# Self attention of a perceiver layer on one core: a tile's row maxima and their way through DRAM directly behind its scores, its subtraction one iteration later, the transposes of the quantized rows later

## The chip, the cores and the metric

The program runs on one core of a Trainium2 chip. The metric is the device time of one execution in microseconds (us); lower is better. TensorE does the matmuls (PE in the profile, PEld its weight loads), VectorE is DVE, ScalarE is ACT, GpSimd is POOL, and SyncE issues most of the DMAs (its queue is SPq).

## The reference

x is 16 batches x 64 queries x 1024. Three residual layers follow one another, each on the layernorm of x:

```
x = x + xattn(layernorm(x), ctx)   # 16 x 1024 context rows, 32 query heads, 8 key/value heads
x = x + attn(layernorm(x))         # self attention: bias, rope, 64 keys per batch
x = x + ffn(layernorm(x))          # int4 rows, ternary weights, relu(gate)^2 * up, int8 rows, down
```

The change lies in the self attention, `softmax(q k^T / sqrt(32)) v` over 64 queries and 64 keys of each batch and head. The feed forward layer begins with this on every row of its input:

```
beta = mean(abs(x)); xq = clip(round(x * sqrt(7) / (beta + eps)), -8, 7)
```

and its gate and up products have 2752 columns each.

## The kernel before

The 1024 rows are eight tiles of 128 (two batches each). The order of all instructions is written out by hand (`tc.manual_schedule()`): each engine, and each DMA queue, works its instructions off in the order in which the program calls them. Work for TensorE that can go anywhere stands as closures in a list, `fillers`; `fill()` (L1055) runs the next one.

The loop of the self attention (L1255) has nine iterations, t = 0 to 8. In iteration t, `two` is tile t and `last` is tile t-1. What the calls issue:

- `by_key(t)` (L773): 32 small matmuls into `w`, four PSUM banks, then two ACT copies (L791) to the tile's 2048 scores per row in SBUF.
- `maxima(t)` (L797), in two halves: a DVE transpose of 32x32 blocks into `blocks2` (L800) and a DVE reduction (L801). What is subtracted in the end is one number for each column (a head and a query), the maximum over the keys, which lie on the partitions.
- `row(t)` (L808): eight small DVE transposes (L813), a small reduction (L817), then on SP's queue a DMA to DRAM (L821) and two DMAs that spread it back over the partitions into `shift2` (L825), 512 KB each. `shift2` lies in the place of `blocks2`.
- `subtract(t)` (L829): one DVE instruction (L830) that waits for those DMAs. `exponentials(t)` (L832): one ACT instruction (L833), in place.
- `values(t)` (L835): 64 matmuls into `w` (L841, L852), which need the exponentials; then three ACT copies.
- `finish(t)` (L868): twelve transposes on TensorE, a DVE reciprocal (L878), two DVE multiplications (L883), and one POOL addition to the residual (L889).
- `quantize(t)` (L912) gives four pieces for the feed forward layer's input, all of them mainly on DVE: `statistics` (L187 to L191, with a power on POOL, L193), `magnitude` (L179, L921), `scaled` (L924 to L927), `rounded` (L930, L932, and the small POOL operations L933, L934). The rounded tile has one buffer.
- `transpose3(t)` (L938): eight TensorE transposes of the rounded tile (L941) into one of two PSUM banks "t0" and "t1", which take turns, and an ACT copy (L942) to `xqT[t]`.

The fillers in iterations 0 to 3 are those of the projection of the second half of the rows: four half chunks of keys, four value steps, then sixteen half chunks of queries, called q1 to q16 below. After each second half a chunk goes through `rotary` (L712): ACT L719, DVE L720 and L721, POOL L722 and L723. From iteration 4 the fillers are 32 gate/up steps (`gate_up`, L952), called g0 to g31: sixteen matmuls each, three ACT operations (L967, L969, L970) and a POOL multiplication (L971). The first twelve go by tiles 0 and 1, then tile 2, then tile 3, each with the column chunks 0 to 2, so that g6 is the first of tile 2, g9 the first of tile 3, and g12 the first of chunk 3. After a chunk's step on tile 3 (g9, g10, g11, g15, ...) `fetch` puts the weights of the chunk three later on SP's queue (L949), two DMAs of 344 KB into the buffers just left. So g12 needs the fetch that is issued behind g9.

Both kinds of filler take PSUM banks from `four_tile` (L94), which goes round m0, m1, t0, t1. An even gate/up step takes t1 and m0, an odd one m1 and t0. Counted through the code, the turns give `transpose3(2)` t0 and `transpose3(5)` t1, before and after the change.

How one iteration runs over these calls, for t from 1 to 7 (two halves of one line each):

```
by_key(t) | fill | exponentials(t-1), maxima(t, 0) | fill | transpose3(t-2), values(t-1), maxima(t, 1) | fill
finish(t-1), row(t) | then fill and a piece of quantize(t-1), three or four times, subtract(t) behind the second piece
```

For t up to 4 there are three of these last steps (all four pieces are issued), later four. In iteration 5 `transpose3(3)` stands behind the first fill. From iteration 1 on, q1 to q6 fall into iteration 1, q7 to q12 into 2, q13 to q16 into 3. Two gate/up steps stand ahead of `by_key(4)`; g2 to g7 follow in iteration 4, g8 to g14 in 5, g15 to g21 in 6, g22 to g28 in 7, g29 to g31 in 8. Behind the loop come the remaining gate/up steps, with the pieces of `quantize(7)` and other work at fixed numbers of steps (`beside`, L1321), among them `transpose3(7)` behind step 8 (L1325); step 9 is the first that uses its tile.

Of the kernel before, what the change touches and what calls it, by code (L numbers as in the profile page):

```python
# [25 lines left out]
NT = B * NQ // P  # L26
# [23 lines left out]
def kernel(  # L50
# [33 lines left out]
    def t_tile(shape, dtype, name, n=None):  # L84

        turns["t"] ^= 1
        n = turns["t"] if n is None else n
        return ps_t.tile(shape, dtype, tag=f"t{n}", name=name)
# [5 lines left out]
    def four_tile(name):  # L94

        turns["four"] = (turns["four"] + 1) % 4
        if turns["four"] < 2:
            return ps_m.tile([P, 512], F32, tag=f"m{turns['four']}", name=name)
        return t_tile([P, 512], F32, name, turns["four"] - 2)
# [812 lines left out]
    def quantize(t):  # L912

        xn = place(xn3_at, [DIM])
        statistics, normalize = layernorm(xn, xs[t], f"n3_{t}")
        b = beta[:, t : t + 1]
        rb = small.tile([P, 1], F32, tag="rb", name=f"rb_{t}")

        def magnitude():
            normalize()  # L920
            nc.vector.tensor_reduce(b, xn, AX.X, ALU.add, apply_absolute_value=True)  # L921

        def scaled():
            nc.vector.tensor_scalar_mul(b, b, 1.0 / DIM)  # L924
            nc.vector.tensor_scalar_add(rb, b, EPS)
            nc.vector.reciprocal(rb, rb)
            nc.vector.tensor_scalar(xn, xn, SQRT7, rb, ALU.mult, ALU.mult)  # L927

        def rounded():
            nc.vector.tensor_scalar(xn, xn, -8.0, 7.0, ALU.max, ALU.min)  # L930
            xq3[t] = place(xq_at, [DIM], BF)
            nc.vector.tensor_scalar(xq3[t], xn, MAGIC, MAGIC, ALU.add, ALU.subtract)  # L932
            nc.gpsimd.tensor_tensor(cgate[:, t : t + 1], b, wscale[:, 0:1], ALU.mult)  # L933
            nc.gpsimd.tensor_tensor(cup[:, t : t + 1], b, wscale[:, 1:2], ALU.mult)  # L934

        return [statistics, magnitude, scaled, rounded]

    def transpose3(t):  # L938
        tp = t_tile([P, KC, P], BF, f"xqp_{t}")
        for k in range(KC):  # L940
            nc.tensor.transpose(tp[:, k, :], xq3[t][:, bass.ts(k, P)], ident_b)  # L941
        nc.scalar.copy(xqT[t], tp)  # L942

    def fetch(n):

        wbs[n] = []
        for i in range(2):
            q = wb_ring.next([KC, CW], F8)
            nc.sync.dma_start(q.rearrange("p k o -> p (k o)"), ternary[i][n % NCH])  # L949
            wbs[n].append(q)  # L950

    def gate_up(n, t, banks, scalar=False):  # L952

        c = n % NCH
        relu, prod = relu_ring.next([CW]), prod_ring.next([CW])
        for i in range(2):
            ps = banks(i)
            for k in range(KC):
                nc.tensor.matmul(  # L959
                    ps[:, :CW],  # L960
                    lhsT=xqT[t][:, k, :],
                    rhs=wbs[n][i][:, k, :],
                    start=(k == 0),
                    stop=(k == KC - 1),
                )
            if i == 0:
                nc.scalar.activation(relu, ps[:, :CW], AF.Relu, scale=cgate[:, t : t + 1])  # L967
        if scalar:
            nc.scalar.activation(prod, ps[:, :CW], AF.Copy, scale=cup[:, t : t + 1])  # L969
            nc.scalar.activation(relu, relu, AF.Square)  # L970
            nc.gpsimd.tensor_tensor(inter[t][:, bass.ts(c, CW)], prod, relu, ALU.mult)  # L971
            return
        nc.vector.scalar_tensor_tensor(
            prod, ps[:, :CW], cup[:, t : t + 1], relu, ALU.mult, ALU.mult
        )
        nc.gpsimd.tensor_tensor(inter[t][:, bass.ts(c, CW)], prod, relu, ALU.mult)
# [78 lines left out]
    def fill(n=1):  # L1055
        for _ in range(n):
            if fillers:
                fillers.pop(0)()

    with tc.manual_schedule():  # L1060
# [14 lines left out]
        unit, last = Unit(0, kT, v), None  # L1075
# [22 lines left out]
        for n in range(2 * B):  # L1098
# [27 lines left out]
            for i in range(4):  # L1126
# [25 lines left out]
                t = n // 4 - 1  # L1152
# [62 lines left out]
            last, unit = unit, following  # L1215
# [38 lines left out]
        two, last = None, None  # L1254
        for t in range(NT + 1):  # L1255
            two, last = (Tile2(t, w) if t < NT else None), two
            late = t >= NT // 2
            if t == NT // 2 - 2:
                for n in range(2):
                    fetch(n)  # L1260
            if t == NT // 2:
                fill(len(fillers))
                fetch(2)
                steps = [(n, tt) for n in range(NCH) for tt in range(NT // 2)]

                steps[:12] = [
                    (n, tt) for tiles in ((0, 1), (2,), (3,)) for n in range(3) for tt in tiles
                ]

                def beside(n, tt):  # L1270
                    gate_up(n, tt, lambda i: four_tile(f"gu_{n}_{tt}_{i}"), scalar=True)
                    if tt == NT // 2 - 1:
                        fetch(n + 3)

                fillers += [lambda s=s: beside(*s) for s in steps]
            if t == NT // 2:
                fill(2)
            pieces = quantize(t - 1) if last and two else []

            def piece():  # L1280
                if pieces:
                    pieces.pop(0)()

            if two:
                two.by_key()
            fill()
            if t == NT // 2 + 1:
                transpose3(t - 2)
            if last:
                last.exponentials()  # L1290
            if two:
                two.maxima(0)
            fill()
            if t > 1 and t != NT // 2 + 1:
                transpose3(t - 2)
            if last:
                last.values()
            if two:
                two.maxima(1)
            fill()  # L1300
            if last:
                last.finish()
            if two:
                two.row()
            for n in range(4):
                if n == 3 and two and t <= NT // 2:
                    break
                fill()
                piece()
                if n == 1 and two:  # L1310
                    two.subtract()
            while pieces:
                piece()
        fill(len(fillers))
# [6 lines left out]
        beside = {9 + 2 * i: step for i, step in enumerate(sum(map(quantize8, range(4)), []))}  # L1321
        beside[0] = fetch_down
        for i, piece in enumerate(pieces):
            beside[(1, 2, 4, 5)[i]] = piece
        beside[8] = lambda: transpose3(NT - 1)  # L1325
        for t in range(2):
            for i, step in enumerate(transpose8(t)):
                beside[14 + 8 * t + 2 * i] = step
# [94 lines left out]
```

## Time and profile before

| | us |
|---|---|
| median of 3 runs | 1886.26 (1885.81 to 1888.18) |
| the profiled execution's own time | 1885.72 |
| its span (first to last instruction) | 1883.9 |
| TensorE busy in the span | 1828.3 |
| mean granted TensorE clock | 0.991 |
| start of `by_key(1)` | 1509.1 |
| start of the last reciprocal L878 (iteration 8) | 1714.7 |

The iterations can be told apart by the DVE reciprocal L878, which comes once in each, at the end of the twelve TensorE transposes of `finish`: it starts at 1524.18, 1551.33, 1578.64, 1607.27, 1637.58, 1665.58, 1689.60 and 1714.72 us in iterations 1 to 8.

The timeline of an engine lists its instructions in order of time: the start, the time from the first start to the last end, the engine and line, what is written from what, how many there are, and in square brackets how long the engine sat idle ahead of them and which instruction released it.

### The profile page before, as it was taken

The numbers are of one execution on the slowest core, as the hardware profiler recorded it, in microseconds if no ns is written. First come the engines' busy times: TensorE is split into PE (matmuls) and PEld (weight loads), VectorE is DVE, ScalarE is ACT, GpSimd is POOL, SyncE is SP. The second block draws the span as 40 slices with busy tenths as digits, with TensorE's granted clock in tenths as the row PEclk, the third lists the DMA queues.
The fourth block names the chain that finished last, engine by engine and source line by source line (L and its number), as shares of the span: only waits on it lengthen the run. The fifth ranks groups of instructions, "written<-read, shape, count | busy, mean of one in ns | idle before, by whom it ended". The sixth has DMA issues, their size and how long they took to land.

```text
span 1883.9 us, 26367 instructions
## 1 busy us (share of the span) xinstructions
PE 1828.3 (97%) x10880; PEld 1083.4 (58%) x10880; DVE 1224.9 (65%) x1436; ACT 928.1 (49%) x988; POOL 872.5 (46%) x479
## 2 busy tenths in 40 slices
PE   8999999999899999999999999999999998889999
PEld 5445556565565665666666666664445544555654
DVE  3012688777777887878878878877523377565564
ACT  1233666656566766766766766543100134563221
POOL 1000457646574674674674665664412334334420
PEclk9999999999999999999999999999999999899999
DMA  9234569777677877877877867743020022334201
GB/s 342 75 103 149 183 226 268 210 242 252 167 241 219 258 227 222 257 228 226 252 227 231 250 224 212 193 174 150 5 89 0 12 65 61 72 88 126 73 29 51
DMA packets 65928, 314.65 MB, mean 167 GB/s; under 512 B 10192, under 2 KB 19344, under 8 KB 49040
## 3 DMA queue, kind: packets, MB, share of 16 engines
q1 hardware_dynamic: 56592, 252.15, 38.2%
q0 software_dynamic: 8064, 58.72, 15.6%
q10 hardware_dynamic: 1152, 2.10, 0.3%
q8 instruction: 85, 1.39, 0.3%
q14 instruction: 35, 0.29, 0.0%
HBM read 293.74 MB, written 19.20 MB: 166 GB/s over the span
## 4 chain that ended last, share of the span: by engine, by line
PE 65%; DVE 4%; DMA 3%; issue 1%; ACT 1%; POOL 0%; SPq 0%; DVEq 0%; POOLq 0%; ACTq 0%
PE v L426 16%; PE z L407 10%; PE wo L250 6%; PE t L575 5%; PE o L637 5%; PE d L1038 4%; PE q L250 4%; PE g L959 4%; PE p L407 4%; DMA arena<-tops 2%; PE k L250 1%; PE v L740 1%; PE gu L959 1%; DVE arena L830 1%; PE w L841 1%
## 5 line engine op out<-in xcount | busy, mean ns | idle before, releaser
L628 POOL TENSOR_TENSOR arena<-arena 128x1024 f32<-128x1024 f32 x192 | 541.9, 2822 | 20.5 <-ACT arena L619 8.5
L426 PE MATMUL v<-arena 128*128 128x256 f32 x1792 | 405.2, 382 | 1.2 <-ACT arena L442 1.2
L594 DVE TENSOR_TENSOR arena<-t,arena 128x512 f32<-128x512 f32 x384 | 258.8, 687 | 211.3 <-PE t L575 155.0
L426 PEld LDWEIGHTS v<-arena 128*128 128x128 f32 x1792 | 336.8, 190 | 78.3 <-issue 29.2
L618 DVE TENSOR_TENSOR arena<-arena 128x2048 f32<-128x2048 f32 x128 | 373.5, 2957 | 4.6 <-DMA arena<-tops 4.6
L587 ACT COPY arena<-t 128x1024 f32<-128x1024 f32 x256 | 254.8, 1009 | 209.6 <-PE t L575 116.3
L619 ACT ACTIVATE arena<-arena 128x2048 f32<-128x2048 f32 x128 | 244.6, 1911 | 168.8 <-DVE arena L618 168.0
L625 POOL TENSOR_TENSOR arena<-arena 128x1024 f32<-128x1024 f32 x32 | 76.4, 2388 | 523.5 <-ACT arena L619 499.2
L407 PE MATMUL z<-arena 128*128 128x512 f32 x560 | 260.0, 606 | 12.1 <-DMA arena<-in_ctxT 8.9
L250 PE MATMUL q<-arena 128*128 128x512 f32 x512 | 224.3, 595 | 0.6 <-ACT arena L287 0.6
L407 PEld LDWEIGHTS z<-arena 128*128 128x128 f32 x560 | 103.0, 191 | 138.8 <-issue 118.1
L250 PEld LDWEIGHTS q<-arena 128*128 128x128 f32 x512 | 95.7, 190 | 117.7 <-issue 115.2
L575 PE MATMUL t<-arena 32*128 32x256 f32 x2048 | 146.7, 400 | 1.2 <-ACT arena L346 1.1
L591 DVE TENSOR_REDUCE arena<-t 128x512 f32<-128x1024 f32 x64 | 74.7, 1204 | 89.8 <-PE t L575 89.8
L959 PEld LDWEIGHTS <-arena 128*128 128x128 bf16 x1024 | 99.2, 98 | 58.8 <-issue 5.0
L575 PEld LDWEIGHTS t<-arena 32*128 32x128 f32 x2048 | 93.1, 184 | 66.6 <-issue 61.4
L637 PE MATMUL o<-arena 128*32 128x256 f32 x2048 | 123.8, 382 | 0.0
L250 PE MATMUL wo<-arena 128*128 128x512 f32 x256 | 112.3, 595 | 0.3 <-ACT arena L287 0.3
L407 PE MATMUL p<-arena 128*128 128x512 f32 x224 | 108.2, 605 | 0.0
L637 PEld LDWEIGHTS o<-arena 128*32 128x32 f32 x2048 | 60.0, 109 | 68.7 <-issue 32.0
L722 POOL TENSOR_TENSOR arena<-arena 128x512 f32<-128x512 f32 x20 | 35.5, 1777 | 122.7 <-DVE arena L720 122.7
L959 PE MATMUL gu<-arena 128*128 128x344 fp8e4 x544 | 85.7, 316 | 1.1 <-ACT arena L942 1.1
(145 smaller groups left out, 1969.4 us busy)
## 6 DMA issues: line engine op xcount, KB each, us to landing
arena<-in_ctxT SPq DMA_DIRECT2D x31, 2048.0 KB, 12.0
arena<-in_ctxT POOLq DMA_DIRECT2D x56, 1024.0 KB, 11.5
arena<-in_ctxT SPq DMA_DIRECT2D x28, 1024.0 KB, 10.5
arena<-tops SPq DMA_DIRECT2D x48, 512.0 KB, 5.0
arena<-in_wg SPq DMA_DIRECT2D x32, 688.0 KB, 4.4
arena<-in_wu SPq DMA_DIRECT2D x32, 688.0 KB, 6.4
arena<-in_wd SPq DMA_DIRECT2D x32, 688.0 KB, 8.7
arena<-ternary SPq DMA_DIRECT2D x32, 344.0 KB, 3.7
```

The source lines that it names most:

```text
L250: nc.tensor.matmul(made[0], lhsT=lhsT(k), rhs=rhs(k), start=(k == 0), stop=(k == KC - 1))
L407: nc.tensor.matmul(held[n], lhsT=weights[:, k, :], rhs=what()[:, k, :], start=(first and k == 0), stop=(k == 3), skip_group_check=not first,)
L426: nc.tensor.matmul(held[n][:, bass.ts(at, KVD)], lhsT=ctx_halves[b, h][:, k, bass.ts(kts[at], P)], rhs=wkvs[:, k, KVD:], start=(k == 0), s ...
L575: nc.tensor.matmul(ws[jj // 2][:, jj % 2, a, :], lhsT=self.kT[rows, self.g, bass.ts(i * 2 + a, P)], rhs=two_tiles[self.b // 2 % 2][rows, s ...
L587: nc.scalar.copy(pt[:, 2 * mine : 2 * mine + 2], ws[mine])
L594: nc.vector.tensor_tensor(m, w[:, :, a], m, ALU.max)
L618: nc.vector.tensor_tensor(pt, pt, by.to_broadcast([P, 4, 2, 256]), ALU.subtract)
L619: nc.scalar.activation(pt, pt, AF.Exp)
L625: nc.gpsimd.tensor_tensor(acc, pt[:, :, 0], pt[:, :, 1], ALU.add)
L628: nc.gpsimd.tensor_tensor(acc, acc, pt[:, :, a], ALU.add)
L637: nc.tensor.matmul(self.po[bass.ts(jj, HD), 0:256], lhsT=self.v[:, kt, bass.ts(self.g * 4 + jj, HD)], rhs=self.pts[i][:, jj, a, :], start= ...
L959: nc.tensor.matmul(ps[:, :CW], lhsT=xqT[t][:, k, :], rhs=wbs[n][i][:, k, :], start=(k == 0), stop=(k == KC - 1),)
```

## The change

It moves calls within the loop and adds or takes away no instruction. `subtract` of a tile goes from the end of its own iteration to the top of the next. Both `maxima` and `row` go directly behind `by_key`. `transpose3(t-2)` goes from ahead of `values` to behind the fill that follows `finish` (in iteration 5 it stays where it was). Exponentials and values keep their places among the fills: behind the first and the second one after `by_key`. One of the fills that had a piece of `quantize` behind it now stands ahead of `transpose3` without one. Behind the loop, `transpose3(7)` comes one step earlier.

```diff
+            if last:
+                last.subtract()
             if two:
                 two.by_key()
+                two.maxima(0)
+                two.maxima(1)
+                two.row()
             fill()
+
             if t == NT // 2 + 1:
                 transpose3(t - 2)
             if last:
                 last.exponentials()
-            if two:
-                two.maxima(0)
+            fill()
+            if last:
+                last.values()
+            fill()
+            if last:
+                last.finish()
             fill()
             if t > 1 and t != NT // 2 + 1:
                 transpose3(t - 2)
-            if last:
-                last.values()
-            if two:
-                two.maxima(1)
-            fill()
-            if last:
-                last.finish()
-            if two:
-                two.row()
-            for n in range(4):
-                if n == 3 and two and t <= NT // 2:
+            for n in range(3):
+                if n == 2 and two and t <= NT // 2:
                     break
                 fill()
                 piece()
-                if n == 1 and two:
-                    two.subtract()
             while pieces:
                 piece()
...
-        beside[8] = lambda: transpose3(NT - 1)
+        beside[7] = lambda: transpose3(NT - 1)
```

## The prediction

> **What bounds the kernel now.** The page first: TensorE is busy nearly throughout, so a gain can only be time in which it stands still or runs slow.
>
> ```profile
> PE 1828.3 (97%) x10880; PEld 1083.4 (58%) x10880; DVE 1224.9 (65%) x1436; ACT 928.1 (49%) x988; POOL 872.5 (46%) x479
> ```
>
> Next TensorE's timeline over the loop. It stands still ahead of `transpose3` (L941) in every iteration from 2 to 8, and once behind it:
>
> ```profile
> 1543.78 0.62 PE L941 MATMUL xqp<-ident_b,arena 128*128 128x128 bf16 x8 [1.29 <-DVE arena L932]
> ...
> 1598.09 1.01 PE L941 MATMUL xqp<-ident_b,arena 128*128 128x128 bf16 x8 [5.57 <-ACT arena L969]
> 1599.03 1.96 PE L841 MATMUL w<-arena 64*32 64x256 f32 x32
> ...
> 1625.18 1.03 PE L941 MATMUL xqp<-ident_b,arena 128*128 128x128 bf16 x8 [7.47 <-DVE arena L932]
> 1627.32 4.50 PE L959 MATMUL gu<-arena 128*128 128x344 fp8e4 x16 [1.10 <-ACT arena L942]
> ```
>
> The waits are 1.29, 1.45, 5.57, 7.47, 1.10, 3.94, 2.49 and 3.43: 26.7 us, and 1.10 more ahead of step 9 behind the loop. Then VectorE's timeline says why (iteration 5 into 6):
>
> ```profile
> 1645.52 1.22 DVE L921 TENSOR_REDUCE beta<-arena 128x1 f32<-128x1024 f32 x1
> 1650.97 2.29 DVE L830 TENSOR_TENSOR arena<-arena 128x2048 f32<-128x2048 f32 x1 [4.22 <-DMA arena<-tops]
> ...
> 1655.18 0.69 DVE L930 TENSOR_SCALAR arena<-arena 128x1024 f32<-128x1024 f32 x1
> 1655.91 0.69 DVE L932 TENSOR_SCALAR arena<-arena 128x1024 bf16<-128x1024 f32 x1
> ```
>
> The subtraction waits for the row's way through DRAM, and the rounding that `transpose3` needs queues behind it. After the longer waits TensorE also runs slow: granted clock 0.50 here, and L841 takes 1.96 instead of 1.09.
>
> ```profile
> 1599.00:1603.00 4.00, 4.00 (x67) 1.78 (x67) 3.38 (x3) 1.21 (x2) 0.41 (x1) 0.50 0.00 0
> ```
>
> (Stretch, its length, five engines' busy time, then the clock.) Iteration 4 pays 2.85 for it (L941 0.39, L841 0.87, L852 0.89, the next gate/up step 0.70), iterations 5, 6 and 8 2.4, 2.6 and 1.4; after 1.29, 1.45 and 2.49 nothing.
>
> **The change, iteration by iteration.** I reckon from one reciprocal L878 (called R, one per iteration) to the next. TensorE goes on 0.27 before R. Removed everywhere: the waits above. Added: the exponentials now wait for a subtraction that stands behind all of `quantize`, so `values` does.
>
> What queues behind the waiting instructions: behind the exponentials on ACT the clearing of the second fill's banks, which TensorE asks for only two steps later (a step takes two of four); behind `maxima` and `row` on DVE the rotary of the fills, which reach POOL a little later and are read an iteration on; behind L821 on SP the fetches (iteration 6 below).
>
> *Iteration 1*: `quantize` hasn't begun; the subtraction is done by about 1512, its exponentials by 1514, and `values` runs at 1517. Nothing.
>
> *Iteration 2.* q6 now has its rotary ahead of `magnitude`, so DVE order is rotary, magnitude, scaled, rounded, subtract. From the end of q6 (1534.3): 0.9 for ACT L719, 1.4 for L720 and L721, 2.05 for L179 and L921, 3.5 to 4.1 from L924 to L932, 2.3 for L830, 1.95 for L833: 12.1 to 12.7. Cover is `by_key` and two fills, 1.05 + 7.1 = 8.15; 3.9 to 4.5 are TensorE idle. `values` starts at 1546.7 instead of 1544.33: **+2.4**.
>
> *Iteration 3.* From R, q10 to q12 take until 10.1. `transpose3(0)` now stands behind q10: 0.55, and by the turns of banks it gets the one q10 fills, so it waits for ACT L719, 0.85. Then 12.4 again, and 7.0 from `values` to R (1544.33 to 1551.33): 30.9 instead of 27.3: **+3.6**.
>
> *Iteration 4.* q16's rotary holds `statistics` until R+5.5, L921 ends at 10.7 (rows of 1584 to 1589), then 4.5 (L924 to L932, as at 1593), 2.3 and 1.95: `values` at 19.4. TensorE gets there at 15.8 (3.3 for q16, 2.0 for `transpose3(1)` and its copy, since g0 takes the same bank, four steps of 2.37, `by_key` 1.05), a wait of 3.6. With 5.84 to the next R: 25.3 instead of 28.6: **-3.3**.
>
> *Iteration 5.* `transpose3(2)` waits 0.65 for the bank of g5, and g6 needs its copy: g6 starts 2.3 after g5. TensorE meets `transpose3(3)` at R+12.5, L932 ends at 12.65; the copy holds g9 to 14.7 and `values` to 17.1, when the exponentials end too. 22.95 instead of 30.3: **-7.4**.
>
> *Iteration 6*, counted from iteration 5's R, and the queue that the row is moved past. `row(5)` is now called ahead of g8, so the fetch behind g9 stands behind it on SP. That was the other way round:
>
> ```profile
> 1629.83 6.68 SPq L949 DMA_DIRECT2D arena<-ternary  x4
> 1640.86 0.32 SPq L821 DMA_DIRECT2D tops<-arena  x1
> 1643.56 1.09 SPq L825 DMA_DIRECT2D arena<-tops  x2
> 1644.70 6.01 SPq L949 DMA_DIRECT2D arena<-ternary  x4
> ```
>
> `row(5)` ends, from iteration 4's R: subtraction done 14.9, two maxima 4.9, row 1.65: 21.4. The write to DRAM takes 1.5 till L825 (2.7 once), the fetch is issued 1.15 later, at 24.1, and lands 7.1 on (the pair issued at 1644.70; pairs behind a spread took 6.4 to 8.7, alone 2.9 to 3.4): 31.2. g12 is due at 25.05: **6.1 of waiting**. So from this R: g12 starts at 8.3, three steps, `by_key`, two steps 12.85, and 5.84: 27.0 instead of 28.0: **-1.0**. The exponentials (16.8) hide beneath.
>
> *Iterations 7 and 8*: L921 ends at R+9.1 (1665.58 to 1674.7), L924 to L932 take 3.4 (1679.73 to 1683.1), L830 and L833 2.3 and 1.95: 16.8; TensorE is there at 15.5 (in 8 at 16.1, since g26 waits 1.7 for `transpose3(5)`'s copy in its bank). Each 16.8 + 5.84 = 22.6 instead of 24.0 and 25.1: **-1.4, -2.5**. The row lands before its subtraction (21.4 + 9 after R, needed a full iteration on).
>
> *Behind*: `transpose3(6)` +0.5; step 9's wait of 1.10 goes, as `transpose3(7)` comes 2.35 earlier and rounding is done by then (R+17 against 19): **-0.6**.
>
> *The clock.* The periods of before hold their slow time; the new ones must be given theirs. Waits of about 4.2, 4.2, 3.6 and 6.1 lie beyond 2.49, which cost nothing, and around 3.43, which did. I take 2.0, 2.0, 1.7 and 2.6 (2.4 each, less for the odds): **+8.3**; bounds 0 and 11.4 (four of 2.85).
>
> The Trainium skill ("TensorE: Matmul & The Clock Gate", section "What's actually happening") says that the clock halves after an idle window of some 3.4 us and recovers after a busy one, the windows running free. The rows agree, with the 3.94 wait slow for longer than one window. By one window for each wait its sum would be four times 1.7, 6.8. The rule speaks against this change: it trades short early waits for long ones.
>
> **Sum**: 2.4 + 3.6 - 3.3 - 7.4 - 1.0 - 1.4 - 2.5 - 0.6 + 8.3 = -1.9. Against the profiled execution's own 1885.72 that is 1883.8; it stands 0.54 below the median of the runs shown, so 1884.3.
>
> Unknowns: the landing 6.4 to 8.7 after issue (-0.7 to +1.6); the DVE chain of iterations 2 and 3 0.3 either way; waits for banks, not seen for these pairs, from 0 (the bank is free) to the 1.1 of g9 and the 5.57 of `transpose3(2)` before: I take the ACT rows that must end, -3 to +3 in all; the clock -8.3 to +3.1. Together the forecast's own range is 1880 to 1889.
>
> **Rivals.** *The fetch is in time* (the row ends early enough, or the landing is as short as alone). For it: 2.9 to 3.4 alone; against: half a megabyte twice ahead of it. It takes away 6.1 and 2.6 and gives back the exponentials' 1.6: -9, 1877.
>
> *Every wait and slow spell goes and nothing takes its place*: 26.7 + 1.1 + 9.3, less a few us of turns: 1852. Against it stands VectorE's order in iterations 2 to 4. Halfway, with the fetch in time and no fall of the clock either (another -5.7), 1871.
>
> *Slower: VectorE becomes the bound.* From R through `quantize`, subtraction and exponentials to the next R is now a ring (12.5 + 4.3 + 5.84) that TensorE waits for in iterations 2, 3, 4, 7 and 8, so each us more on VectorE is paid five times. Operations there come in two lengths: L179 0.81 and 1.39, L927 1.20 and 1.40, L930 0.69 and 1.64, L932 0.69 and 1.29, the long ones partly beside POOL work. In iterations 2 to 4 up to 1.8 more each could come, in 7 and 8 up to 1.5, 8 in all: 1892. It decides from 1.1 an iteration on (5.6 turn -1.9 into +3.7).
>
> *It doesn't do what it says*: it is announced as moving exponentials and values one gate/up step later too. Counted in fills they stay (first and second behind `by_key`), so no time is gained for them; the sum has it so.
>
> **Numbers.** Forecast 0.60, fetch in time 0.17, slower ring 0.16, waits gone 0.07. A measurement of this kernel can tell 0.2%, 3.8 us. Inside the forecast's case 0.22 falls below that, 0.68 within and 0.10 above; so faster 0.13 + 0.17 + 0.07 = 0.37, within 0.41, slower 0.06 + 0.16 = 0.22. The range takes in the fetch in time and most of the slower ring, and leaves out the waits gone: 1875 to 1891. Cases of both signs are in it; the likeliest one's own is 1880 to 1889.
>
> **What the profile would show.** TensorE's waits for L932 gone from 6 to 8; waits ahead of L841 for ACT L833 of some 4 in iterations 2 and 3, 3.6 in 4, 1.4 and 0.7 in 7 and 8; one of some 6 ahead of g12 for a DMA from `ternary`; L821 some 20 us earlier against R, L949 behind L825 in iteration 5; clock 0.5 after these. The prediction is wrong if `values` doesn't wait in 2 and 3, or g12 doesn't wait.

## The result, and the profile after

The changed kernel takes 1892.28 us (median of 7 runs, 1890.39 to 1893.51), the kernel before in the same comparison 1885.81: a ratio of 1.0033, 95% interval [1.0022, 1.0045]. It is slower by 6.5 us; forecast were -1.9, and the range ended at 1891. The profiled execution has a span of 1889.3 us, 5.4 more than before.

TensorE's line of the changed kernel's page shows nothing of it, as busy time takes in the slow stretches:

```profile
PE 1829.8 (97%) x10880; PEld 1083.4 (57%) x10880; DVE 1222.9 (65%) x1436; ACT 927.0 (49%) x988; POOL 875.8 (46%) x479
```

TensorE's timeline over the loop does (start, time, instruction, and in brackets the idle time ahead and its releaser):

```profile
1546.14 1.96 PE L841 MATMUL w<-arena 64*32 64x256 f32 x32 [4.11 <-ACT arena L833]
...
1607.94 1.96 PE L841 MATMUL w<-arena 64*32 64x256 f32 x32 [3.95 <-ACT arena L833]
...
1630.01 0.62 PE L941 MATMUL xqp<-ident_b,arena 128*128 128x128 bf16 x8 [1.71 <-DVE arena L932]
...
1649.34 8.51 PE L959 MATMUL gu<-arena 128*128 128x344 fp8e4 x48 [5.53 <-DMA arena<-ternary]
...
1713.41 1.96 PE L841 MATMUL w<-arena 64*32 64x256 f32 x32 [2.91 <-ACT arena L833]
```

The waits for rounding (L932) ahead of the transposes are gone but one; `values` (L841) waits for the exponentials instead, and g12 for its weights. Before, 25.7 us of TensorE's waits stood ahead of L941 (20.1 for L932, 5.6 for L969). The view of waits of the changed kernel (total, times, longest) begins:

```profile
PE w L841 <- ACT arena L833: 18.6, 6, 4.2
PE gu L959 <- DMA arena<-ternary: 5.5, 1, 5.5
PE gu L959 <- ACT arena L942: 5.0, 4, 1.5
```

From 1500 to 1760 us the brackets add up to 32.4 us; before they were 27.8 (the loop's 26.7 and the 1.10 ahead of step 9). The slow clock stands behind six of the waits instead of four; for instance, in the table by stretch (granted clock third from the end):

```profile
1608.00:1611.00 3.00, 3.00 (x64) 1.52 (x64) 2.96 (x5) 1.14 (x3) 0.91 (x1) 0.50 0.00 0
```

From reciprocal to reciprocal (forecast: with its share of the clock):

| to iteration | before | forecast | measured |
|---|---|---|---|
| 2 | 27.2 | 31.6 | 31.1 |
| 3 | 27.3 | 32.9 | 33.4 |
| 4 | 28.6 | 27.0 | 27.1 |
| 5 | 30.3 | 23.0 | **26.3** |
| 6 | 28.0 | 29.6 | 29.6 |
| 7 | 24.0 | 22.6 | 23.2 |
| 8 | 25.1 | 22.6 | **26.5** |
| behind | 169.2 | 168.6 | 168.4 |

Two rows carry the miss: 3.3 and 3.9 of the 7.7 us too much. The place is found on VectorE. Its timeline in iterations 5 and 6 of the changed kernel, from the statistics to the subtraction:

```profile
1647.27 0.15 DVE L191 TENSOR_SCALAR ve_n<-mv_n 128x1 f32<-128x1 f32 x1
1655.70 0.81 DVE L179 TENSOR_SCALAR arena<-arena,mv_n,rs_n 128x1024 f32<-128x1024 f32 x1 [8.28 <-POOL rs_n L193]
...
1661.11 2.27 DVE L830 TENSOR_TENSOR arena<-arena 128x2048 f32<-128x2048 f32 x1
```

VectorE has the variance at 1647.4 and gets the power of it, one element per row, more than 8 us later. POOL's timeline says what stands ahead of that power:

```profile
1645.62 0.93 POOL L971 TENSOR_TENSOR arena<-arena 128x344 f32<-128x344 f32 x1
1654.25 0.91 POOL L971 TENSOR_TENSOR arena<-arena 128x344 f32<-128x344 f32 x1 [7.70 <-ACT arena L970]
1655.12 0.55 POOL L193 TENSOR_TENSOR rs_n<-ve_n,neg_half 128x1 f32<-128x1 f32 x1
```

It is the multiplication of one more gate/up step (here g12, which waits for its weights). The change puts a fill without a piece behind `finish`, so `statistics` is called one step later, and on POOL's queue its power stands behind that step's L971. VectorE's waits from 1590 to 1725, before and then after, show how the wait of the subtraction for its DMA is exchanged for one for that power:

```profile
DVE arena L830 <- DMA arena<-tops: 14.1, 5, 4.2
...
DVE arena L179 <- POOL rs_n L193: 2.7, 4, 0.7
```

```profile
DVE arena L179 <- POOL rs_n L193: 18.7, 5, 8.3
```

From the reciprocals of iterations 4 to 7, L179 starts 6.5 us later before the change and 9.7, 14.1, 7.6 and 9.3 after it. The following iteration's subtraction, exponentials and `values` hang on it.

### The profile page after: what moved, and what is told of

Its sections match the earlier page's. It is cut to its first block, busy times and chain, and to the rows that moved or that the text cites. A ratio compares the mean times of both kernels' runs of the same rounds, so it can differ in the third digit from the quotient of the medians.

```text
span 1889.3 us, 26379 instructions
## 1 busy us (share of the span) xinstructions
PE 1829.8 (97%) x10880; PEld 1083.4 (57%) x10880; DVE 1222.9 (65%) x1436; ACT 927.0 (49%) x988; POOL 875.8 (46%) x479
## 4 chain that ended last, share of the span: by engine, by line
PE 67%; DVE 3%; ACT 1%; DMA 1%; issue 0%; POOL 0%; ACTq 0%; DVEq 0%
PE v L426 16%; PE z L407 10%; PE wo L250 6%; PE q L250 5%; PE t L575 5%; PE o L637 5%; PE d L1038 4%; PE g L959 4%; PE p L407 4%; PE gu L959 2%; PE k L250 1%; PE v L740 1%; DVE arena L830 1%; PE w L841 1%; ACT arena L833 1%; PE o L647 1%
## 6 DMA issues: line engine op xcount, KB each, us to landing
arena<-in_ctxT POOLq DMA_DIRECT2D x56, 1024.0 KB, 11.4
```

## The experiments

The theory: the forecast's mechanisms are right, and what failed is the length of VectorE's chain from 5 on, because its power queues on POOL. The rival was on record: VectorE itself is slower (long forms, L930 and L830 among them). Then come single parts of the change, done alone and undone, since the change gives back more than the removed waits were worth; one of these, maxima and row undone, was not run. Each ratio is to the kernel before.

**Statistics one step earlier** (in the changed kernel).

```diff
                 last.finish()
             fill()
+            piece()
             if t > 1 and t != NT // 2 + 1:
...
                 fill()
-                piece()
+                if n:
+                    piece()
```

> The changed kernel with the statistics piece of quantize issued one gate/up step earlier (behind the fill that follows finish, ahead of transpose3); the other pieces stay. Theory POOL: the power L193 of the layernorm stands on POOL behind the multiplication L971 of one more gate/up step than before, and that step waits for a transpose copy (iterations 5, 8) or for the late fetch (6). Then L179 comes 6.5 us after the reciprocal again in iterations 5 to 8 instead of 9.7, 14.1, 7.6 and 9.3, and about 3.3 + 1.7 + 0.5 + 3.5 us go: some 1883 to 1885. Rival VectorE: the ring is long because L930 and L830 take their long forms (1.28, 3.02); moving a piece that holds none of them changes nothing, 1892.

Measured 1882.27, ratio 0.9982 [0.9972, 0.9991]: ten us less than the change. L179 comes 6.5 us after all four reciprocals (the expectation counts them by the iteration that uses them). The periods to iterations 5 to 8 are 23.3, 28.1, 22.6 and 22.5; 22.95, 22.6 and 22.6 had been forecast for 5, 7 and 8. POOL's timeline has the power ahead of g12's multiplication now:

```profile
1642.50 0.93 POOL L971 TENSOR_TENSOR arena<-arena 128x344 f32<-128x344 f32 x1
1644.37 0.55 POOL L193 TENSOR_TENSOR rs_n<-ve_n,neg_half 128x1 f32<-128x1 f32 x1 [0.94 <-DVE ve_n L191]
1650.73 2.08 POOL L971 TENSOR_TENSOR arena<-arena 128x344 f32<-128x344 f32 x1 [5.81 <-ACT arena L970]
```

In iteration 5 the variance (L191) is there 5.85 us after the reciprocal in the kernel before, in the changed one and in this one; only the power's place on POOL's queue differs. VectorE's own speed isn't needed to explain the miss: for iterations 7 and 8 of the changed kernel it takes 7.8 us from L179 to the end of L830, and the rows that the forecast used made that 8.3.

**Row behind the second fill** (in the changed kernel).

```diff
                 two.maxima(1)
-                two.row()
             fill()
...
             fill()
+            if two:
+                two.row()
             if last:
                 last.values()
```

> The changed kernel with row called behind the second fill, so that in iteration 5 the fetch behind g9 stands ahead of the row's DMAs on SP again. Theory SP order: the wait of 5.5 us ahead of g12 goes, and with it the slow clock behind it (1.3): 1885 to 1887. Rival: the fetch is slow because the spread of the row fills the DMA engines, whichever stands first: a wait of 2 us or more ahead of g12 stays, 1889 or more.

Measured 1884.49, 0.9993 [0.9984, 1.0003], just below the expected range. g12 has no wait, and the period to iteration 6 falls from 29.6 to 22.7. SP's queue in iteration 5:

```profile
1634.64 2.15 SPq L949 DMA_DIRECT2D arena<-ternary  x2
1640.05 0.32 SPq L821 DMA_DIRECT2D tops<-arena  x1
1641.47 1.09 SPq L825 DMA_DIRECT2D arena<-tops  x2
```

In the changed kernel the row's DMAs stood first:

```profile
1639.53 0.32 SPq L821 DMA_DIRECT2D tops<-arena  x1
1641.01 1.08 SPq L825 DMA_DIRECT2D arena<-tops  x2
1642.19 3.05 SPq L949 DMA_DIRECT2D arena<-ternary  x6
```

There the first two fetches landed 7.1 to 8.1 us after issue, behind the spread; here the first landed after 2.7 to 3.2. So the order of the calls on SP made g12 wait, as forecast.

**Both edits.**

> Both edits. If POOL's queue and SP's queue are two separate causes, both gains come: the exponentials end 16.9 us after the reciprocal in iterations 5 to 8 and g12 doesn't wait: 1878 to 1880. If the one hides the other, no better than the better of the two, 1884.

Measured 1877.23, 0.9953 [0.9938, 0.9969], just below the expected range's lower end. The periods to 5 to 8 are 23.3, 22.6, 22.6 and 22.5: the two causes are separate, and the ring of 22.6 is what the forecast had worked out. Left are the waits of 4.1, 4.2 and 3.9 in iterations 2 to 4.

**All pieces one step earlier** (as the first edit, but with `piece()` behind every fill of the loop over n as well).

```diff
             fill()
+            piece()
             if t > 1 and t != NT // 2 + 1:
```

> The changed kernel with all pieces of quantize one step earlier (statistics behind the fill after finish, magnitude behind the next, and so on), row as in the change. In iterations 2 and 3 magnitude then stands ahead of the rotary of q6 and q12 on VectorE, as before the change. Theory: what makes values wait 4.1 there is magnitude behind that rotary; the wait falls by 2.05 to 2.0, and the clock no longer falls: 2 x 2 + 2 x 1.8 beyond stats_early, some 1877. Rival: the wait is the subtraction's being behind rounding; magnitude's place changes it by under 1 us, and the result is that of stats_early, 1884.

Measured 1878.37, 0.9972 [0.9955, 0.9989]. The waits in iterations 2 and 3 are 2.45 and 2.51, down by 1.7, so magnitude's place behind the rotary is a large part of them. That the clock wouldn't fall behind them was wrong: L841 and L852 still take 1.60 and 2.01 after the first. The interval overlaps with that of the first edit alone, so the waits show this gain and the time by itself does not.

**Maxima and row alone** (in the kernel before; the subtraction stays behind magnitude).

```diff
             if two:
                 two.by_key()
+                two.maxima(0)
+                two.maxima(1)
+                two.row()
             fill()
...
-            if two:
-                two.row()
             for n in range(4):
```

> The kernel before with one part of the change alone: maxima and row directly behind by_key; subtraction, transposes and pieces stay where they were. The row should then have landed when magnitude ends, so the subtraction no longer waits for its DMA (before 1.0 to 4.2 each time): the waits ahead of transpose3 fall by 1 in iterations 2 and 3, 1.5 in 4, 3 in 5, and go in 6 to 8 with their slow clock. Against it the fetch behind g9 is late by some 4. Theory: 1868 to 1873, so the subtraction's new place is what costs in the change. Rival: early maxima push VectorE's other work back and the waits stay, 1884 or more.

Measured 1868.02, 0.9898 [0.9882, 0.9914]. VectorE no longer waits for the row anywhere in the loop, and in iterations 6 to 8 `transpose3` waits under 1 us, for ACT; waits of 4.0 and 4.3 stay in 4 and 5. This part of the change alone gives 19 us. g12 waits 1.6, less than the 4 expected.

**The same with row behind the second fill.**

> The same with row behind the second fill, so that the fetch stands ahead of it on SP: no wait ahead of g12, otherwise as maxima_row_only: 1864 to 1869. If SP's order is not what makes g12 wait: no difference to maxima_row_only.

Measured 1867.28, 0.9895 [0.9879, 0.9911]. g12's wait of 1.6 is gone in the trace, but the intervals of the two runs overlap almost wholly: no difference can be told.

**The subtraction alone** (in the kernel before).

```diff
+            if last:
+                last.subtract()
             if two:
                 two.by_key()
...
-                if n == 1 and two:
-                    two.subtract()
```

> The kernel before with the other part alone: the subtraction at the top of the next iteration; maxima, row and transposes stay. Rounding is no longer behind it, so transpose3 waits less (2 in iteration 5, 0 later), values waits for the exponentials instead: 1.9 in 6, about 1 in 7 and 8, nothing changed in 2 and 3. By the rows 1866 to 1872. If a subtraction behind rounding is what makes the changed kernel slow by itself: 1886 or more.

Measured 1879.16, 0.996 [0.9945, 0.9976]: better than before, but by less than the rows had said. The view of waits of this kernel names what I had left out:

```profile
PE xqp L941 <- ACT arena L969: 6.5, 1, 6.5
PE xqp L941 <- ACT arena L967: 5.7, 2, 3.2
PE w L841 <- ACT arena L833: 3.2, 2, 2.0
PE xqp L941 <- ACT arena L719: 3.0, 1, 3.0
```

The transposes, still ahead of `values`, take the bank of the second fill, and the clearing of that bank (L967, L969, L719) stands on ACT behind the exponentials. So they wait for the late subtraction too.

**The transposes alone** (in the kernel before).

```diff
             fill()
-            if t > 1 and t != NT // 2 + 1:
-                transpose3(t - 2)
             if last:
                 last.values()
...
                 fill()
+                if n == 0 and t > 1 and t != NT // 2 + 1:
+                    transpose3(t - 2)
                 piece()
...
-        beside[8] = lambda: transpose3(NT - 1)
+        beside[7] = lambda: transpose3(NT - 1)
```

> The kernel before with the third part alone: transpose3 behind the fill after finish, transpose3(7) one step earlier. transpose3 no longer waits for rounding, but values waits for the exponentials behind the same subtraction, and g6 and g26 wait for the copies: by the rows 1875 to 1882. If banks and copies cost more than 4 us in all: no better than before.

Measured 1870.3, 0.9915 [0.9897, 0.9933]: more than expected. The third part alone gives 16 us.

**The change with the subtraction undone** (back behind the piece at n == 1).

> The changed kernel with one part undone: the subtraction back behind the magnitude piece of its own iteration; maxima, row and transposes as in the change. Theory: the subtraction behind all of quantize is what makes values wait for the exponentials (4.1, 4.2, 4.0 in iterations 2 to 4, 1.7 to 2.9 in 6 to 8); with the row early it needs no wait for its DMA either. These waits go, but for 0.5 each in 2 and 3 (rotary ahead of magnitude) and some of 4; a wait ahead of g12 of 2 to 4 stays: 1864 to 1870. Rival: the late power on POOL keeps the ring long wherever the subtraction stands: 1880 or more.

Measured 1870.06, 0.9919 [0.9905, 0.9934], at the range's upper end. The waits ahead of `values` are 1.3, 1.3, 2.5 and three times 0.5, 6.6 in all instead of 18.6:

```profile
PE w L841 <- ACT arena L833: 6.6, 6, 2.5
...
PE xqp L941 <- DVE arena L932: 4.4, 1, 4.4
```

g12 waits only 1.0 (its weight load 1.4, for the fetch), not 2 to 4. The late power stays (L179 at 7.6 to 9.3 after the reciprocals of iterations 4 to 7). In the periods to 7 and 8 it no longer shows (21.95 and 22.48, as in the combined kernel below, where the power is early), since the exponentials don't stand behind rounding; in 5 `transpose3(3)` waits 4.4 for rounding, which stands behind the subtraction again, with some 2.5 of slow rows after it, more than the 1.7 and 1.55 of the change. So the subtraction's place is what makes `values` wait for the late power, and that place alone is worth 22 us between the change and this kernel.

**The change with the transposes undone** (as `subtract_only`, with maxima and row directly behind the scores).

> The changed kernel with another part undone: transposes and the fills of the pieces as before the change; the subtraction at the top and maxima and row behind the scores stay. Statistics are one step earlier by that, as in stats_early, and magnitude stands ahead of the third rotary. Theory: values still waits for the exponentials (2 to 4 in iterations 2 to 4, 1.2 to 1.7 in 7 and 8) and g12 for the fetch (5): 1874 to 1881. If the transposes' new place (copies, banks) were what costs: 1866 or less.

Measured 1885.55, 1.0003 [0.9994, 1.0013]: slower than I expected, for the reason met in `subtract_only`. The transposes wait 3.0, 6.5 and (two waits) 4.2 for banks behind the exponentials, and g12 for the late fetch:

```profile
PE xqp L941 <- ACT arena L969: 6.5, 1, 6.5
PE gu L959 <- DMA arena<-ternary: 5.2, 1, 5.2
PE xqp L941 <- ACT arena L967: 4.2, 2, 3.2
```

With the subtraction late, either place of the transposes costs: the old one these waits, the new one, as the change makes it, the later statistics.

**The parts that pay, together**: maxima behind the scores, row behind the second fill, transposes late, `transpose3(7)` at step 7; the subtraction behind magnitude and the pieces at their old steps.

> The kernel before with maxima directly behind the scores, row behind the second fill, transposes where the change puts them, and the subtraction and the pieces where they were. Theory: neither rounding nor the DMA nor SP's order is waited for, but in iteration 5, where transpose3(3) waits for rounding still (some 4): 1860 to 1865, below each of its parts (1867.3 and 1870.3). If banks and copies give back what the waits save: 1867 or more.

Measured 1859.51, 0.9865 [0.9849, 0.9882], just below the expected range: faster than both kernels, by 26 us and 33. The expected wait of 4 in iteration 5 is 0.8.

**The same with tile 4's subtraction behind its iteration's rounding.**

```diff
-                if n == 1 and two:
+                if n == 1 and two and t != NT // 2:
                     two.subtract()
             while pieces:
                 piece()
+            if t == NT // 2:
+                two.subtract()
```

> The same, and tile 4's subtraction alone behind the rounding of iteration 4, since transpose3(3) in iteration 5 is the one transpose that comes early. Its wait falls from some 4 to some 2, with less slow clock: 2 to 4 us below combined. If exponentials(4) then hold values back instead: no gain.

Measured 1858.35, 0.9854 [0.9838, 0.9871]. The intervals overlap almost wholly: no gain that could be told, as the wait it aims at had been only 0.8.

## Why the prediction was wrong, step by step

- *What bounds the kernel*: right. Between the profiles of before and after, TensorE's waits grow by 4.6 and the slow rows by 1.1, the span by 5.4; from before to the combined kernel they fall by 17.7 and 7.6, the span by 25.7.
- *Iterations 2 and 3* (values waits 3.9 to 4.5 for a subtraction behind rotary, magnitude and rounding; 0.85 for a bank): right; 4.11, 4.18 and 0.86. *Iteration 4* (3.6): 3.95, right.
- *Iteration 6* (g12 waits 6.1 for the fetch behind the row on SP): right in mechanism and nearly in size, 5.53; moving the row removes it. The period came out as forecast, 29.6, by errors against each other: a slow clock of 1.3 instead of 2.6 and a wait 0.6 shorter, but exponentials that did not hide and held `values` 1.68, again behind the late power.
- *Iterations 5, 7 and 8* (-7.4, -1.4, -2.5; measured -4.0, -0.9, +1.4): here it failed. "L921 ends at R+9.1" and, in 5, "L932 ends at 12.65" took VectorE's chain from the trace before, where `statistics` follows the first fill behind `finish`. I had seen that one fill now has no piece, and counted its effect on VectorE (the rotary) but not on POOL, where the power L193 went one multiplication back. Rounding ended at 14.7 in 5, and L921 at 9.7 and 11.4 in 7 and 8. The periods came out 3.3, 0.6 and 3.9 over the forecast, with the slow clock that came with it; putting the power forward took back 3.0, 0.6 and 4.1 there, and 1.5 in 6. The step left uncounted is a moved call's third queue.
- *The slower rival* named the ring and the time, 1892, but another cause: VectorE's long forms. That its time was met is luck: putting the statistics, and with them the power, forward took ten us away.
- *The clock*, +8.3: right in kind. The four waits that it counted cost 7.0, between 1.3 and 2.4 each. Behind all six waits the slow rows of TensorE make some 10.3 us (1.75, 2.4, 1.55, 1.55, 1.3 and 1.75 above their fast forms). Two of them, in iterations 5 and 8, were not in the sum; they belong to the waits that the late power made (with the power put forward these rows are fast).
- *The end* (-0.6): -0.8.

The larger lesson is in the parts: the early maxima and row give 19 us alone, the late transposes 16, and the subtraction's new place, which neither needs, takes more than both back in company, though alone it gives 8: once the row is early, the subtraction has nothing to wait for behind magnitude.

## What to carry to other kernels

When a call is moved past a step, list its instructions engine by engine, and for each one the instruction that now stands directly ahead of it on that engine; here a power of 128 numbers on POOL, 0.55 us of work, held up the whole ring. Move the producer of a late operand first and look whether its consumer still waits, before the consumer is moved as well. Where several moves are made at once, measure each one alone and each one undone: here each paid alone, by 19, 16 and 8 us, and the third, with the other two made, cost 22 where those two together had given 16.

## What the runs showed of the hardware

A wait of a given length does not settle whether TensorE's clock falls. Behind waits of 2.42 and 2.45 us (subtraction alone, pieces early) the next rows were slow, L941 at 1.01 and L841 at 1.60; behind 2.49 (subtraction undone) they were fast, L841 at 1.10. Within one run (transposes alone) L841 took 1.84 behind a wait of 2.06 and 1.10 behind one of 2.86. In the combined kernel slow rows followed waits of 0.70 and 1.10 with one `transpose3` between them (ahead of them only one of 1.24, some nine us earlier): the two gate/up steps behind them took 6.54 instead of 4.87, and the granted clock from 1604 to 1607 was 0.50. The timeline and the table by stretch:

```profile
1603.10 6.54 PE L959 MATMUL gu<-arena 128*128 128x344 fp8e4 x32 [1.10 <-ACT arena L942]
```

```profile
1604.00:1607.00 3.00, 3.00 (x12) 1.61 (x11) 2.23 (x6) 0.55 (x1) 0.85 (x2) 0.50 0.90 188
```

The same pair of waits, 0.69 and 1.10 at 1618 in the changed kernel, had no slow rows behind it (4.87). The Trainium skill ("TensorE: Matmul & The Clock Gate", section "What's actually happening") speaks of an idle window of some 3.4 us; here slow rows followed waits shorter than that, and the measurement decides. Why the same pair of waits has slow rows behind it in one run and not in another is left open.
